# One attention and scan kernel: the drain after the last unit becomes part of the planned order

## The chip, the cores and the metric

The kernel runs on one core of a Trainium2 chip. The metric is the device time of one execution in microseconds (us). Before the change it was 2515.1 us, the median of three runs (2513.02 to 2516.12).

Engines are named as in the profile: PE is TensorE (the matmul array), DVE is VectorE, ACT is ScalarE, POOL is GpSimd, SP is SyncE, which here only issues transfers. Each works through its own queue in order, and an instruction at a queue's head that waits holds up everything behind it.

## What is computed

The reference is one layer: cross attention, then a recurrent scan over time, then two additions. Cut to what matters, with 4096 rows of `x`, 3202 rows of context, width 512, 8 heads of 64 and a state of 64:

```python
xn, kn = layernorm(x, g1, beta1), layernorm(ctx, g1, beta1)
x = x + mha(xn, kn, W_qkv, b_qkv, W_o, b_o)          # softmax over 3202 keys
U = (layernorm(x, g2, beta2) @ W_in.T + b_in) @ Bmat  # 4096 x 64
def step(s, u_t):
    s = silu(s @ A.T) + u_t
    return s, s
_, states = lax.scan(step, zeros(64), U)              # 4096 steps, one after the other
x = x + states @ Cmat
return x + program_probs.mean() @ W_prog.T + b_prog
```

Everything is float32.

## The kernel before

**The attention.** The rows are cut into 8 blocks of 512 (`NQB`), each with 4 pairs of heads (`NC`) and 2 halves of 256 rows: 64 units. A unit runs over 13 double chunks of keys (`NDC`). For each chunk PE makes the scores `s` (L605), ACT copies them to `p` (L618), DVE keeps a running maximum `top` (L633). Once the unit's maximum is known, PE turns it (`tt`, L641), DVE reduces it (`m`, L648) and PE spreads it over the partitions (`mb`, L656). Then, chunk by chunk, DVE subtracts it (`less`, L664), ACT takes the exponential (L674), POOL adds the weights up (`acc`, L682) and PE multiplies by the values (`po`, L691). In the very last unit some chunks aren't added by POOL: PE sums them with a product by ones (`pd`, L708). The variable `PE_SUMS` says which; before, chunks 2, 4, 6, 8, 10 and 12.

**The order of the work.** All of this is entered into a `Plan` (L54) as pieces. A piece has a name, an engine, an estimated cost in ns, the pieces it comes after, a due time, and the buffers that it takes and gives back. `Plan.order` (L92) plays the pieces through with these costs. Whenever an engine is free, it takes the piece that is due first among those that are ready and have buffers, and the list that results is the order in which instructions are issued. So the planner's costs and due times decide only the order on each engine; the chip then runs each queue as fast as its waits allow.

**The scan.** The 4096 steps are cut into 256 stretches of 16 (`L`). The stretches lie side by side, in two groups of 64 states on the 128 partitions, so one matmul by `a_t` advances all of them by a step. A sweep (L1062) is 16 such steps: PE adds the recurrent part to `z` (L1072), ACT takes a tanh (L1085), DVE multiplies it with `z` to `h` (L1086). The inputs' part of `z` comes four steps at a time from `terms` (L1053 to L1057). Sweep a starts every stretch from nothing. Sweep b starts each from the end state that sweep a found for the stretch before it, and from its states POOL forms `s` (L1096), PE the rows `states @ Cmat` (`products`, L1102, tiles `py`, `py_b`, `py_o`), ACT, POOL and DVE join them with the rows that were fetched from DRAM (`row`, L1109 to L1112), and SP stores them. At the end the end states of both sweeps are compared (`differ`, L1128 to L1134); should they differ, a branch repeats the sweeps.

**The last 256 rows.** They belong to the last units, so their attention is finished last, and they have a small scan of their own with stretches of 8 steps: `last_rows` (L1175) takes the last unit's output `o`, multiplies by `W_o` (`py`, L1170), adds the residual (`x_l`, L1187), normalizes (DVE statistics, three short POOL operations, ACT), turns the rows (`tp_yl`, L270), forms the scan's inputs (`pu_l`, L1198), and then makes 24 small steps (`zl`, L1250, tanh L1252, product L1253).

**The drain, before.** The plan ends with the last unit's pieces, the fetches of the rows for sweep b (`row<-x1d`, L1020, 32 transfers on SP's queue) and the first three parts of the last rows' product. After that the order is written by hand. `finish_last` (L716) sums `acc`, takes the reciprocals and scales `o`. Then two generators are advanced in turn: for each `yield` of `last_rows` one step of `main_scan`, which is sweep a and then sweep b with its products, delayed by a step:

```python
for _ in last_rows(ws[len(units) - 1]):
    next(scan, None)
for _ in scan:
    pass
last_outputs("a")
```

In sweep a, PE also gets filler matmuls: two products of a tile of zeros per step (L1078), bf16, 512 columns, whose result nobody reads. Each product of sweep b is one matmul of 512 columns for each of the two groups of states (64 partitions each).

Of the kernel before, what the change touches and what calls it, by code (L numbers as in the profile page):

```python
# [20 lines left out]
P = 128  # L21
# [142 lines left out]
def xattn_ssm_kernel(  # L164
# [37 lines left out]
    zeros = const.tile([P, H], BF16, name="zeros")  # L202
    nc.gpsimd.memset(zeros, 0.0)
# [512 lines left out]
    def finish_last(w):  # L716
        Q, hp, half = w["at"]
        o = op.tile([P, QU], F32, tag="o", name=f"o_{Q}_{hp}_{half}", bufs=12)
        o_t[Q, hp, half] = o
        nc.scalar.copy(o, w["po"][:, 0, :])  # L720
        sums(w["pd"], w["acc"], CK, False, True)
        yield
        rd = op.tile([P, QU], F32, tag="rd", name="rd_last", bufs=1)
        for t in range(2):
            nc.vector.reciprocal(
                rd[:, t * P : (t + 1) * P], w["pd"][:, t * P : (t + 1) * P]
            )
            if t == 0:
                yield
        nc.vector.tensor_tensor(o, o, rd, ALU.mult)  # L730
        yield

# [264 lines left out]
    PE_SUMS = range(2, NDC, 2)  # L997
# [64 lines left out]
    def sweep(start, end, fill=0):  # L1062


        before = None
        for j in range(L):
            if j == 0:
                terms(0, start)
            h = sv["h"][j % 3]
            z = sv["z"][:, j // 4 % 2, j % 4, :]  # L1070
            if before is not None:
                nc.tensor.matmul(z, a_t, before, start=False, stop=True, skip_group_check=True)  # L1072
            if j % 4 == 1 and j + 4 < L:
                terms(j // 4 + 1, None)
            elif fill:

                for _ in range(fill):
                    nc.tensor.matmul(  # L1078
                        sv["fill"], zeros[:, :P], zeros, start=True, stop=True
                    )  # L1080
            if j == 0 and start is None:
                nc.vector.memset(h, 0.0)
            else:
                th = sv["th"][j % 2]
                nc.scalar.activation(th, z, AF.Tanh, scale=0.5)  # L1085
                nc.vector.scalar_tensor_tensor(h, th, 1.0, z, ALU.add, ALU.mult)  # L1086
            before = h
            if j < L - 1:
                yield j, h
        nc.vector.tensor_tensor(end[:, 1:], h, u[:, L - 1, :], ALU.add)  # L1090
        nc.vector.tensor_copy(end[NS:, 0:1], end[:NS, NCK : NCK + 1])
        yield j, h
# [6 lines left out]
    def products(j, s):  # L1099
        for v, n in enumerate(counts):  # L1100
            r = slice(v * NS, (v + 1) * NS)
            nc.tensor.matmul(sv["py"][j % 2][v], s[r, :], sv["c2"][r], start=True, stop=True)  # L1102

    def outputs(j):

        py, t, y = sv["py"][j % 2], rows[j], sv["y"][:, j % 2, :]
        n = counts[1]
        if j % 3 < 2:
            nc.scalar.activation(y, py[1], AF.Copy, scale=0.5)  # L1109
            nc.gpsimd.tensor_tensor(t[:n, 1, :], y[:n], t[:n, 1, :], ALU.add)  # L1110
        for v in range(1 if j % 3 < 2 else 2):
            nc.vector.scalar_tensor_tensor(  # L1112
                t[: counts[v], v, :], py[v][: counts[v]], 0.5, t[: counts[v], v, :],
                ALU.mult, ALU.add,
            )
        nc.sync.dma_start(outr[0, j], t[:, 0, :])
        nc.sync.dma_start(outr[1, j, :n], t[:n, 1, :])
# [7 lines left out]
    def differ(new, old, n, bad):  # L1125

        top, df, ok = sv["top"], sv["df"][:, :n], sv["ok"][:, :n]
        nc.vector.tensor_tensor(df, new, old, ALU.subtract)  # L1128
        nc.vector.tensor_scalar(ok, df, top, None, ALU.is_le)
        nc.vector.tensor_scalar(df, df, -1.0, None, ALU.mult)  # L1130
        nc.vector.tensor_scalar(df, df, top, None, ALU.is_le)
        nc.vector.tensor_tensor(ok, ok, df, ALU.mult)
        nc.vector.tensor_reduce(bad, ok, AX.X, ALU.add, negate=True)
        nc.vector.tensor_scalar(bad, bad, float(n), None, ALU.add)  # L1134

    def main_scan():
        ends = sv["end0"], sv["end1"]
        sv["z"] = ps_s.tile([P, 2, 4, NCK], F32, tag="s", name="z")
        for end in ends:
            nc.vector.memset(end[:NS, 0:1], 0.0)  # L1140
# [4 lines left out]
        yield  # L1145
        for _ in sweep(None, ends[1], 2):
            yield

        s = None
        for j, h in sweep(ends[1][:, :NCK], ends[0]):  # L1150
            if j:
                products(j - 1, s)
            s = states(j, h)
            if j > 1:
                outputs(j - 2)
            yield
        products(L - 1, s)
        largest(ends[0][:, 1:])
        outputs(L - 2)
        yield  # L1160
        differ(ends[0][:, 1:], ends[1][:, 1:], NCK, sv["bad"])
        yield
        outputs(L - 1)
        yield

    def last_products(cs):

        for c in cs:
            for g in range(2):
                nc.tensor.matmul(  # L1170
                    sv["py"][0][g], o_t[NQB - 1, c, 1][:, g * P : (g + 1) * P], wo[:, c, :],
                    start=(c == 0), stop=(c == NC - 1),
                )

    def last_rows(w):  # L1175

        yield from finish_last(w)
        last_products([NC - 1])
        yield
        tiles = range(2)  # L1180
        x1s, scaled, tps, pus = [], [], [], []
        ul, hw, hl, sl, th = (sv[k] for k in ("ul", "hw", "hl", "sl", "thl"))

        def x1_(g):
            x1 = xp_.tile([P, H], F32, tag="x1", name=f"x1_l{g}")
            x1s.append(x1)
            nc.vector.tensor_tensor(x1, sv["py"][0][g], xl[g], ALU.add)  # L1187

        def turn(g):
            tps.append(transposes(ps_m, "m", xhs[g], P, f"yl{g}"))  # L1190

        xns = [sv["xn"][:, g, :].rearrange("p (c k) -> p c k", c=NC) for g in tiles]

        def steps_(g):
            pu = ps_m.tile([P, P], F32, tag="m", name=f"pu_l{g}")
            pus.append(pu)
            for c in range(NC):
                nc.tensor.matmul(  # L1198
                    pu[g * NS : (g + 1) * NS], wc[:, c, :], xns[g][:, c, :],
                    start=(c == 0), stop=(c == NC - 1),  # L1200
                )

        def kept(g):
            hs = slice(g * NS, (g + 1) * NS)
            nc.vector.tensor_scalar(
                ul[hs, PRE + 1 :], pus[g][hs], bu[hs], 2.0, ALU.add, ALU.mult
            )

        xhs = []
        x1_(0)  # L1210
        yield
        scaled.append(normalize(x1s[0], P, "yl0", later=True))
        yield
        x1_(1)
        yield
        xhs.append(scaled[0]())
        scaled.append(normalize(x1s[1], P, "yl1", later=True))
        yield
        turn(0)
        yield  # L1220
        xhs.append(scaled[1]())
        nc.scalar.copy(xns[0], tps[0])
        yield
        turn(1)
        steps_(0)
        yield
        nc.scalar.copy(xns[1], tps[1])
        kept(0)
        nc.vector.tensor_copy(ul[NS:, : PRE + 1], ul[:NS, P:])
        yield  # L1230
        steps_(1)
        for g in tiles:
            nc.gpsimd.tensor_tensor(xl[g], x1s[g], modb, ALU.add)
            nc.sync.dma_start(x1d[LAST + g * P : LAST + (g + 1) * P, :], xl[g])
        yield
        kept(1)

        zl = ps_m.tile([P, PRE // LT + 1, P], F32, tag="m", name="zl")
        for i in range(PRE // LT + 1):
            nc.tensor.matmul(  # L1240
                zl[:, i, :], a_t, ul[:, i * LT : i * LT + P], start=(i == 0), stop=True,
                skip_group_check=True,
            )
        yield
        before = None
        for t in range(PRE + LT):
            i, j = divmod(t, LT)
            z = zl[:, i, j::LT]
            if before is not None:
                nc.tensor.matmul(z, a_t, before, start=False, stop=True, skip_group_check=True)  # L1250
            h = (hl if i == PRE // LT else hw)[:, j::LT]
            nc.scalar.activation(th, z, AF.Tanh, scale=0.5)  # L1252
            nc.vector.scalar_tensor_tensor(h, th, 1.0, z, ALU.add, ALU.mult)  # L1253
            if t == PRE:

                nc.vector.tensor_tensor(sv["st"], hw[:, LT - 1 :: LT], ul[:, PRE :: LT][:, : P // LT], ALU.add)
            before = h
            yield
        nc.vector.tensor_tensor(sl[:, 1:], hl, ul[:, PRE + 1 :], ALU.add)

# [252 lines left out]
```

## Time and profile before

| | us |
|---|---|
| median of three runs | 2515.1 |
| the profiled execution | 2515.3 |
| its span | 2513.5 |
| PE busy | 2418.6 (96%) |
| DVE busy | 2087.6 (83%) |
| POOL busy | 2066.7 (82%) |
| ACT busy | 1922.3 (76%) |
| last `mb`, start | 2410.8 |
| first step of sweep a, its `terms` on PE | 2436.5 |
| first `z` of sweep b | 2462.7 |
| `nbad`, the last operation before the branch | 2507.3 |

The span runs from the first to the last recorded instruction, and the execution's own time is 1.8 us longer. The profile is of one execution, taken on the chip. Its page gives busy times, the granted clock of PE, the chain of work that ended last (followed back from the last instruction), and the costliest groups of instructions by line. The trace behind it can be asked for the timeline of an engine, for waits, and for busy times by windows. `L705` stands for line 705 of the kernel; `po<-p,v` for output and inputs.

### The profile page before, as it was taken

What the parts mean: (1) busy time and instruction counts of PE and PEld (TensorE: products, weight loads), DVE (VectorE), ACT (ScalarE), POOL (GpSimd) and SP (SyncE); (2) the same over time, 40 slices, a digit from 0 to 9 for tenths busy, and PEclk for the clock granted to TensorE, in tenths of its full rate; (3) what the DMA queues carried; (4) which work ended last, traced back from release to release, by engine and by line L of the source; (5) the groups of instructions that cost most, each with busy time, mean ns of one, the idle gap of its engine ahead of it and who ended that gap; (6) DMA issues with size and microseconds to landing.
All of it is one profiled execution on the core that took longest, in us unless ns stands there. A gap on an engine that the chain in (4) does not pass through costs nothing.

```text
span 2513.5 us, 43994 instructions
## 1 busy us (share of the span) xinstructions
PE 2418.6 (96%) x16390; PEld 1409.1 (56%) x16392; DVE 2087.6 (83%) x2242; ACT 1922.3 (76%) x2373; POOL 2066.7 (82%) x1195
## 2 busy tenths in 40 slices
PE   7999899999999999999999999999999999999987
PEld 3444555655565555655565556555565556555543
DVE  2220699999999989899999999999989899999964
ACT  2222588878987898788987898789878888888852
POOL 1110299989998999899998999899989999899963
PEclk9999999999999999999999999999999999999998
DMA  3422322112211222122211221222212221233364
GB/s 120 131 99 79 88 64 62 45 48 68 66 56 53 66 66 66 49 62 85 64 49 43 68 78 46 60 67 67 58 48 67 74 64 53 83 115 118 107 165 144
DMA packets 178035, 189.21 MB, mean 75 GB/s; under 512 B 14252, under 2 KB 151256, under 8 KB 177818
## 3 DMA queue, kind: packets, MB, share of 16 engines
q1 hardware_dynamic: 173270, 178.67, 23.7%
q10 hardware_dynamic: 4548, 7.67, 1.0%
q8 instruction: 133, 2.18, 0.4%
q14 instruction: 84, 0.69, 0.1%
HBM read 156.40 MB, written 29.89 MB: 74 GB/s over the span
## 4 chain that ended last, share of the span: by engine, by line
PE 38%; DVE 22%; POOL 17%; issue 13%; ACT 6%; DMA 2%; SPq 1%; ACTq 0%; POOLq 0%; DVEq 0%
POOL acc L682 15%; DVE top L633 12%; PE s L605 12%; PE po L691 9%; DVE p L664 6%; ACT p L618 3%; PE pv L534 3%; PE pk L560 3%; PE pq L294 3%; PE pa L900 2%; ACT p L674 2%; PE tt L641 1%; POOL both L747 1%; PE pd L753 1%; DMA cx<-in_ctx_dram 1%
## 5 line engine op out<-in xcount | busy, mean ns | idle before, releaser
L682 POOL TENSOR_TENSOR acc<-p,acc 122x1024 f32<-122x1024 f32 (+1 forms) x698 | 1653.0, 2368 | 60.7 <-ACT p L674 17.9
L664 DVE TENSOR_TENSOR p<-p,mb 123x1024 f32<-123x1024 f32 (+2 forms) x832 | 991.7, 1208 | 23.2 <-PE mb L656 23.2
L674 ACT ACTIVATE p<-p 123x1024 f32<-123x1024 f32 (+2 forms) x832 | 875.4, 1058 | 138.9 <-DVE p L664 134.2
L618 ACT COPY p<-s 123x1024 f32<-123x1024 f32 (+2 forms) x832 | 829.6, 1006 | 168.4 <-PE s L605 121.6
L605 PE MATMUL s<-q,k 64*123 64x256 f32 (+2 forms) x6656 | 911.1, 398 | 25.2 <-DVE top L633 15.0
L691 PE MATMUL po<-p,v 123*64 123x256 f32 (+2 forms) x6656 | 877.5, 390 | 6.6 <-ACT p L674 4.7
L633 DVE TENSOR_TENSOR top<-s,top 123x1024 f32<-123x1024 f32 (+1 forms) x640 | 777.3, 1215 | 11.5 <-ACT p L618 9.3
L605 PEld LDWEIGHTS s<-q,k 64*123 64x123 f32 (+2 forms) x6656 | 574.9, 182 | 337.7 <-DVE top L633 115.9
L691 PEld LDWEIGHTS po<-p,v 123*64 123x64 f32 (+2 forms) x6656 | 423.5, 136 | 357.9 <-issue 145.5
L682 POOL TENSOR_TENSOR acc<-p,p 124x1024 f32<-124x1024 f32 x64 | 152.3, 2380 | 121.2 <-DMA k<-kd 73.8
L633 DVE TENSOR_TENSOR top<-s,p 124x1024 f32<-124x1024 f32 x64 | 78.2, 1222 | 99.3 <-ACT p L618 66.3
L294 PE MATMUL pq<-xn,wq 128*128 128x256 f32 x512 | 126.7, 390 | 0.0
L243 POOL TENSOR_SCALAR ve_c<-mv_c 123x1 f32<-123x1 f32 (+2 forms) x26 | 6.1, 233 | 145.7 <-DVE mv_c L236 117.8
L900 PE MATMUL pa<-wo,o 128*128 128x512 f32 x240 | 116.9, 609 | 0.0
L504 DVE COPY ct<-tp_c 128x492 f32<-128x492 f32 (+2 forms) x13 | 8.7, 672 | 123.3 <-PE tp_c L270 123.3
L294 PEld LDWEIGHTS pq<-xn,wq 128*128 128x128 f32 x512 | 92.2, 189 | 31.6 <-issue 21.2
L568 ACT ACTIVATE ks<-pk,bias 128x492 f32<-128x492 f32 (+3 forms) x28 | 18.0, 643 | 118.6 <-PE pk L560 58.4
L534 PE MATMUL pv<-wv,ct 128*123 128x512 f32 (+2 forms) x208 | 99.0, 621 | 0.0
L560 PE MATMUL pk<-ct,wk 128*128 128x492 f32 (+3 forms) x224 | 89.1, 550 | 0.0
L747 POOL TENSOR_TENSOR both<-acc 124x512 f32<-124x512 f32 x63 | 80.8, 1283 | 3.0
L648 DVE TENSOR_REDUCE m<-tt 128x4 f32<-128x496 f32 x64 | 42.9, 671 | 42.7 <-PE tt L641 42.7
L534 PEld LDWEIGHTS pv<-wv,ct 128*123 128x123 f32 (+2 forms) x208 | 39.1, 196 | 46.0 <-issue 45.1
(196 smaller groups left out, 1486.3 us busy)
## 6 DMA issues: line engine op xcount, KB each, us to landing
k<-kd SPq DMA_DIRECT2D x324, 123.0 KB
v<-vd SPq DMA_DIRECT2D x324, 123.0 KB
k<-kd SPq DMA_DIRECT2D x108, 124.0 KB
v<-vd SPq DMA_DIRECT2D x108, 124.0 KB
xr<-in_x_dram SPq DMA_DIRECT2D x32, 256.0 KB
x1d<-xr SPq DMA_DIRECT2D x32, 256.0 KB
x<-in_x_dram SPq DMA_DIRECT2D x28, 256.0 KB
cx<-in_ctx_dram SPq DMA_DIRECT2D x18, 246.0 KB
```

The costliest lines, as they stand in the source:

```text
L294: nc.tensor.matmul(pq[:, half * QU : (half + 1) * QU], wq[:, i, hp * P : (hp + 1) * P], xns[half][:, i, :], start=(i == 0), stop=(i == NC ...
L534: nc.tensor.matmul(pv[:n, :H], ct[:, i, o : o + n], wv[:, i, :], start=(i == 0), stop=(i == NC - 1),)
L560: nc.tensor.matmul(pk[:, :n_g], wk[:, i, hp * P : (hp + 1) * P], ct[:, i, :n_g], start=(i == 0), stop=(i == NC - 1),)
L605: nc.tensor.matmul(s[:n, a, b, :], kts[(*w["at"][:2], c)][r, b * n : (b + 1) * n], q[r], start=True, stop=True,)
L618: nc.scalar.copy(t[:n], w["ps"][c][:n])
L633: nc.vector.tensor_tensor(w["top"][:n], s[:n], before[:n], ALU.max)
L664: nc.vector.tensor_tensor(t[:n], t[:n], w["mb"][:n].unsqueeze(2).to_broadcast([n, 2, 2, QU]), ALU.subtract,)
L674: nc.scalar.activation(t[:n], t[:n], AF.Exp)
L682: nc.gpsimd.tensor_tensor(w["acc"][:n], t[:n], before[:n], ALU.add)
L691: nc.tensor.matmul(w["po"][a * HD : (a + 1) * HD, 0, :], vts[(*w["at"][:2], c)][:n, b, a * HD : (a + 1) * HD], t[:n, a, b, :], start=(c == ...
L747: nc.gpsimd.tensor_tensor(w["both"], acc[:, :, 0, :], acc[:, :, 1, :], ALU.add)
L900: nc.tensor.matmul(v["pa"], o_t[Q, c, t // 2][:, t % 2 * P : (t % 2 + 1) * P], wo[:, c, :], start=(c == 0), stop=(c == NC - 1),)
```

## The change

The hand-written part goes. `finish_last`, `main_scan` and the interleaving loops are replaced by pieces of the plan with names, costs, predecessors and due times, so that the planner decides their order together with the last unit's softmax. In particular:

- sweep a is entered with a pace of 1500 ns a step and a due time of three `STEP` (2600 ns each) behind the last unit's scores. Its only predecessor is `start`, which makes the scan's tiles ready; nothing ties it to the end of the last unit
- the last unit's sums, reciprocals and scaling, the last rows and their small scan, and sweep b at 1900 ns a step follow with due times from 16 `STEP` on
- `PE_SUMS` becomes chunks 4, 8 and 12; POOL adds 2, 6 and 10
- a product of sweep b is entered in two parts of 256 columns, so it is four matmuls instead of two, between which other pieces can stand
- the scaling of the last `o`, the last product by `W_o` and the comparisons are cut into smaller pieces
- the fillers and the tile of zeros are removed

```diff
-    PE_SUMS = range(2, NDC, 2)
+    PE_SUMS = (4, 8, 12)
+    A_PACE, B_PACE = 1500, 1900
...
-    def sweep(start, end, fill=0):
...
-            elif fill:
-                for _ in range(fill):
-                    nc.tensor.matmul(
-                        sv["fill"], zeros[:, :P], zeros, start=True, stop=True
-                    )
...
+    def sweep(k, start, end, d=0, pace=0, after=()):
...
+        for j in range(L):
+            q = j // 4
+            if j % 4 == 0:
+                free = [(k, "h", 4 * q - 5)] if q > 1 else list(after)
+                yield (k, "terms", q), "PE", 950, partial(terms_, q), free, d - 3 * pace if q else d
+            if j or start is not None:
+                if j:
+                    yield (k, "z", j), "PE", 300, partial(z_, j), [(k, "terms", q), (k, "h", j - 1)], d
+                yield (
+                    (k, "tanh", j), "ACT", 280, partial(tanh_, j),
+                    [(k, "z", j) if j else (k, "terms", 0)], d + 400,
+                )
+                free = [("states", j - 3)] if j > 2 and start is not None else []
+                yield (k, "h", j), "DVE", 290, partial(h_, j), [(k, "tanh", j)] + free, d + 800
...
+            d += pace
+        yield (k, "end"), "DVE", 450, last_, [(k, "h", L - 1)], d
...
+    def last_unit(plan, w, n, d):
...
+        plan.add("l.copied", "ACT", 370, copied, [("product", n, NDC - 1)], d, ["o_"])
+        plan.add("l.summed", "PE", 860, summed,
+                 [("add", n, last)] + [("sums", n, c) for c in PE_SUMS], d, [], [], "product")
+        for t in range(2):
+            plan.add(("l.inverse", t), "DVE", 950, partial(inverse, t), ["l.summed"], d + t,
+                     [] if t else ["wide"], [("m", ("sums", n, PE_SUMS[0]))])
+            plan.add(("l.over", t), "DVE", 290, partial(scaled_, t), ["l.copied", ("l.inverse", t)], d + t)
...
+        for p in sweep("a", None, "end1", d + 3 * STEP, A_PACE, ["start"]):
+            plan.add(*p)
+        d += 16 * STEP
+        last_unit(plan, ws[n], n, d)
+        last_rows(plan, d)
+        for p in sweep("b", "end1", "end0", d + STEP, B_PACE, [("a", "end")]):
+            plan.add(*p)
...
+            for part in range(2):
+                plan.add(("products", j, part), "PE", 590, partial(products_, j, part),
+                         [("states", j), *free[j % 2]], e + 1000 + part)
...
-        sv["fill"] = sv["py"][1][0]
-        for _ in last_rows(ws[len(units) - 1]):
-            next(scan, None)
-        for _ in scan:
-            pass
-        last_outputs("a")
-        differ(sv["sl"][:, : P : LT], sv["st"], P // LT, sv["badl"])
```

The computation stays the same, apart from the order of the sums in the last unit's denominators. The branch that repeats the sweeps is rewritten to the new form of `sweep`, with the same steps.

## The prediction

> **What bounds the kernel now.** I read the page first. PE is busy 96% of the span, and the first 2400 us are the planned order, which the change leaves alone: by the listing of both built programs, each engine's instructions agree up to the last unit's softmax. So only the last 110 us matter, and there I read the chain of work that ended last:
>
> ```profile
> 2434.89 1.73 PE pd L708 x16
> ...
> 2440.56 0.44 DVE o L730
> ...
> 2458.03 0.94 PE zl L1240 x6
> ...
> 2462.74 0.49 PE z L1056 x2
> ...
> 2495.33 0.39 PE py_b L1102
> ...
> 2502.22 2.13 PE py_a L1267 x4
> ```
>
> Columns: start, length, engine, tile, line. Four stages follow from it. S1, from the end of the last `mb` (2411.85, PE's timeline) to the end of the sum over `acc`, the last group of `pd` (2436.5): 24.6 us. S2, sweep a and the first half of the last rows, to sweep b's first `z` (2462.74): 26.3. S3, sweep b with its products, to the end of the last product (2495.72): 33.0. S4, to the end of `nbad` (2507.5): 11.8. Then 6.0 to the end of the span.
>
> Next the timeline, for the price of a step:
>
> ```profile
> 2443.94 0.49 PE L1072 MATMUL z<-scan,a_t 128*128 128x128 f32 x2 [0.26 <-DVE scan L1086]
> ...
> 2445.12 0.49 PE L1072 MATMUL z<-scan,a_t 128*128 128x128 f32 x2 [0.26 <-DVE scan L1086]
> ...
> 2470.35 0.40 PE L1250 MATMUL zl<-scan,a_t 128*128 128x16 f32 x2
> 2470.60 0.47 PE L1072 MATMUL z<-scan,a_t 128*128 128x128 f32 x2
> 2470.99 0.69 PE L1102 MATMUL py_b<-c,scan 64*128 64x512 f32 x1
> ```
>
> A bare sweep step (`z`, tanh, product, next `z`) takes 2445.12 − 2443.94 = 1.18. On a busy PE a `z` takes 0.25 when the next matmul has the array's same shape, but 0.39 (2470.60 to 2470.99) when the next one uses half of it: 0.14 for the change of shape. On POOL's own timeline five additions to `acc` take 12.17 from 2419.01, 2.43 each.
>
> Last, PE by windows (window, length, busy, instructions, granted clock, DMA share, GB/s):
>
> ```profile
> 2401.57:2404.98 3.41, 1.66 (x12) 1.00 0.22 76
> 2404.98:2408.39 3.41, 3.08 (x10) 0.50 0.20 69
> ...
> 2439.11:2442.52 3.41, 2.40 (x8) 1.00 1.06 252
> ...
> 2493.72:2497.13 3.41, 2.06 (x10) 1.00 0.76 255
> ```
>
> The clock halves after a window with 1.66 or 2.06 busy (the next one's clock is 0.50 both times), not after one with 2.40.
>
> **The change part by part.** Ahead of S1 nothing moves the path: `mb` stands behind one group of `py` in both orders. The dropped memset of `zeros` has no row of its own; the nearest, a DVE memset, takes 0.17, on a POOL that is idle for most of the first 150 us: nothing, at most 0.2.
>
> *Sweep a into S1.* PE gains 15 `z` x 0.25 = 3.75 and four terms, 0.66 + 3 x 0.87 = 3.3. It loses three of six chunk sums, 3 x 0.87 = 2.6 (their chunks go to POOL). Changes of shape rise from 7 to 25, 18 x 0.14 = 2.5. PE's work grows by 6.9: 24.6 + 6.9 = 31.5, to 2443.4.
>
> Each step also puts a wait into three queues: `z` on PE (the next `po` stands behind), tanh on ACT (the next exp), the product `h` on DVE (the next subtraction). In the new order five `h` stand between the subtractions and ten behind the last. The subtractions end at 2411.89 + 13 x 1.13 + 5 x 0.21 + 0.8 (`rd`) + 0.35 (`o`) = 2428.8, 1 us later than now. From there `z`7 to `z`15 take seven steps with a `po` between them, 0.25 + 0.14 + 0.86 + 0.14 = 1.39, longer than the bare 1.18 and so PE's, and one with terms, 2.04 as at 2445.12 to 2447.16: 11.8. Then `z`15 and three groups, 0.4 + 2.6: 2443.9. The two sums agree; with half a microsecond for imperfect fit, 2444.4. **S1: +8.0.** The cover: POOL does nine additions, its last ending at 2419.01 + 8 x 2.43 = 2438.5 where now it ends at 2431.2. The sum over `acc` is due at 2443.5, so these 7.3 us are hidden by 5; were sweep a free, S1 could still not end before 2439.4, +2.9.
>
> Tanh among exps: both orders hold one load of ACT's function set, at the start, so no switch is paid. ACT is busy 14.6 of the 26 us from 2411 and gets 15 x 0.28 = 4.2.
>
> *S2 disappears.* Sweep b's first `z` follows the sum directly. The 26 filler matmuls, 0.215 each, go with it. **−26.3.**
>
> *S3 takes the last rows.* Now: 16 `z` (4.0), terms (3.3), 16 products of 0.92 (14.7), 16 small steps `zl` (3.8), 31 changes of shape (4.3), sum 30.1, and 2.9 of waiting, mostly for DVE's joins `row` (two in a row, 1.28). After: besides, the last `py` 1.9, transposes 0.9, `pu` 2.0, terms of the small scan 0.8, two small steps more, 48 changes: 38.0, +7.9. Half-width products: a block becomes four of 256 columns, the shape of the scores, 16 records in 1.99, 8 in 0.99 with its change of shape; the full width took 1.06 with its own. I take no difference; worse by 0.14 a step they would cost 2.2, better by 0.07 they would give 1.1.
>
> The waiting grows. DVE holds both reciprocals (0.95 each) and the scalings back until the sum is there: `o` at 2446.9. From `o` to the terms of the small scan it took 17.0 (2441.0 to 2458.0); the rows' bare chain (`py` 0.95, `x1` 0.68, statistics 0.87, POOL 1.25, 0.81, transposes 0.5, 0.56, `pu` 1.0, the second tile 3.2 behind, 0.8) is some 11; middle 14, so 2460.9 = 16.5 after S3's start. By the new order five `z` of sweep b but only four products stand before that. Behind it PE still has 12 products (10.6), 11 `z` (2.75), terms 1.7, 18 small steps 4.3, some 36 changes 5.0: 24.4; and 11 steps wait, at twice today's 0.18 a step since 1.6 small steps now stand in DVE's queue per step: 4.1. S3: 16.5 + 24.4 + 4.1 = 45.0. **+12.0.**
>
> SP: the 32 fetches keep their place (2415 to 2441.6, DMA share 1.07); the stores moved ahead start near 2450, so they collide with nothing, and 7.7 MB have 40 us where they had 30. The two stores of `xr` stand among them and nobody waits.
>
> *S4.* Five small steps at 1.10 (2499.70 to 2500.80), the states 0.3, `py_a` 2.1, two joins and a remnant of the comparison 1.6, `pbad` and `nbad` 0.6: 10.1. The first comparison, seven operations, 2 us on DVE, no longer stands between two small steps (1.62 idle before `zl`), and most of the second lies beside `py_a`. **−1.7.**
>
> Sum: 8.0 − 26.3 + 12.0 − 1.7 = −8.0. The profiled execution took 2515.3 (span 2513.5), within 0.2 of the median of three, 2515.1. 2515.3 − 8.0 = **2507.3 us**.
>
> **Rules weighed.** The Trainium skill, "TensorEngine Tiling (Array Packing)", Key Properties, says that a change of tiling mode drains the array, which speaks against half-width products with `z` and `zl` in between. The row prices the drain at 0.14; 35 more changes make 4.9, counted above. The rule gives no figure; the gain would be gone at 0.14 + 8.0/35 = 0.37 a change, which no row shows.
>
> "TensorE: Matmul & The Clock Gate" (Why this matters for your kernels) fears idle gaps above some 3 us. By it nothing happens here, fillers or not: no gap of this walk reaches 2 us. By the row the clock fell after gaps no longer than 1.53, in a window half busy. The row decides: the stretch around 2447 to 2452, where sweep b waits for the last rows, may fall. It is a rival below.
>
> **The rivals.** *PE alone decides.* The queues add no waiting beyond today's: +6.9 − 26.3 + 7.9 − 1.7 = −13.2, **2502.1**. For it: sweep steps with fillers between ran at 1.18. Against: 17 us from `o` to the small scan.
>
> *The clock halves once in early S3.* The fall at 2404.98 made `po` 1.98 for 1.08, `py` 3.78 for 1.98, `mb` 1.06 for 0.64: 3.1. Then −4.9, **2510.4**. For it: only four products in 16 us. Against: `pu`, `py` and the terms are dense there, and 2.40 of 3.41 was enough.
>
> *Slower: the coupled queues.* A late `h` on DVE holds `z`, the matmuls behind it, the joins behind those and so the next `h`. Place: the 9 steps at the end of S1 and the 16 of S3. Each 0.1 us more a step costs 2.5. From 0.32 a step the gain is gone, at 0.52 the kernel takes 2515.3 − 8.0 + 13.0 = **2520.3**. For it: a step with one `pu` group in between took 1.94 (2454.60 to 2456.54), 0.55 over mine. Against: that step also had a filler, and PE was simply full.
>
> That the change does not do what it says is excluded: the listing shows the `z` between the `po`.
>
> **How the numbers follow.** Likeliest 0.53 (its own range 2505 to 2510), PE alone 0.17, the clock 0.20, slower 0.08, something unseen 0.02. About 0.2%, 5 us, can be told from no change: faster, below 2510.3, holds the first two and a little under half of the third, 0.76; same 0.16; slower 0.08. The range 2502.0 to 2512.5 leaves out the slower case and half of the edges.
>
> **What would show it.** `acc`'s sum ending near 2444 with POOL's last addition near 2438; sweep b's first `z` right behind it; terms of the small scan near 2461; the last product near 2489.5; granted clock 1.00 from 2412 to there. Wrong would be: `z` in S1 over 1.6 apart, POOL ending last, S3 above 48, or a window at 0.50 between 2447 and 2461.

## The result, and the profile after

The changed kernel takes 2509.7 us, the median of 20 runs (2505.8 to 2512.18); the kernel before 2514.8, the median of 20 (2512.38 to 2516.82). The ratio is 0.9979, with a 95% interval of 0.9973 to 0.9986: 5.1 us faster, where 7.8 were forecast. The profiled execution took 2511.05, with a span of 2509.2; that is 4.25 less than the profiled execution of before.

The chain of the changed kernel, at the places that were shown of the kernel before (start, length, engine, tile, line):

```profile
2444.13 0.89 PE pd L706 x8
...
2446.73 0.24 DVE o L1197
...
2461.78 0.86 PE zl L1264 x6
...
2490.89 1.08 PE py L1102 x4
...
2499.04 2.13 PE py_a L1325 x4
```

The order is turned round. Sweep a is gone from behind `pd`. From the end of `o` to the small scan's terms it is 14.8 us, where it was 17.0, and the 30.2 us from these terms to the end of the last product hold sweep b, its products and the small steps together.

The stages, cut as in the prediction, from PE's and DVE's timelines. S1 runs from the end of the last `mb` to the end of the sum over `acc`, S2 to sweep b's first `z`, S3 to the end of the last product, S4 to the end of `nbad`. The experiments, named below, stand in the same table:

| kernel | S1 | S2 | S3 | S4 | `mb` to `nbad` | median |
|---|---|---|---|---|---|---|
| before | 24.8 | 26.1 | 33.0 | 11.7 | 95.6 | 2514.8 |
| forecast | 32.8 | 0 | 45.0 | 10.0 | 87.6 | 2507.3 |
| after | 33.5 | 0 | 47.0 | 11.0 | 91.5 | 2509.7 |
| sweep a late | 28.2 | 24.9 | 42.5 | 5.9 | 101.5 | 2521.9 |
| six sums on PE | 37.0 | 0 | 44.7 | 11.0 | 92.8 | 2515.0 |
| products whole | 33.5 | 0 | 41.2 | 18.2 | 92.9 | 2509.8 |
| work in sweep b | 33.5 | 0 | 44.5 | 11.0 | 88.9 | 2507.8 |
| the same, and at the end | 33.5 | 0 | 44.4 | 11.2 | 89.0 | 2508.4 |
| before, no fillers | 24.9 | 26.8 | 35.9 | 11.7 | 99.3 | 2522.7 |
| late rows on DVE | 33.5 | 0 | 48.1 | 10.0 | 91.6 | 2510.3 |
| work in sweep b, late rows | 33.5 | 0 | 43.4 | 10.2 | 87.0 | 2505.6 |
| the same, and at the end | 33.5 | 0 | 43.4 | 9.4 | 86.2 | 2504.9 |
| work, late rows, two sums | 32.6 | 0 | 43.4 | 10.2 | 86.1 | 2505.5 |

The forecast row adds the prediction's differences to the row of before (its S2 would come out at −0.2). With six sums, sweep b starts ahead of the sum, so S3 is counted from the sum's end. The stages are those of one profiled execution, the median is that of all runs. They need not move alike: the last `mb` ends anywhere from 2407 to 2414 in these profiles, in a part of the program that is the same in all of them, so stages are compared by their lengths and not by absolute times. The experiments were timed in three groups (the first four, the next four, the last three, as they stand below), each with the kernel before, whose medians were 2514.9, 2514.2 and 2515.1. So differences of medians between groups are good to about 1 us, and the ratio to the kernel before, given with its 95% interval, compares better.

S1 is the length that repeats best, 33.5 in seven kernels. S3 carries the difference. PE by windows there (window, length, busy, instructions, granted clock, DMA share, GB/s):

```profile
2449.35:2452.76 3.41, 1.64 (x12) 1.00 0.00 0
2452.76:2456.18 3.42, 3.42 (x16) 0.60 0.45 143
...
2476.65:2480.07 3.42, 2.50 (x18) 1.00 0.42 148
2480.07:2483.48 3.41, 3.41 (x18) 0.60 0.73 237
```

Twice in S3 the clock falls to 0.50 for the length of one such stretch (the first time from 2453.4 to 2456.8; a window that mixes it with full clock shows 0.60). Each time the stretch ahead has waits in it: 1.28 and 0.49 in the first, for DVE's `h` and POOL's states, and 0.53 and 0.39 in the second.

```profile
2451.56 0.49 PE L1052 MATMUL z<-scan,a_t 128*128 128x128 f32 x2 [1.28 <-DVE scan L1065]
2452.54 0.70 PE L1102 MATMUL py<-c,scan 64*128 64x256 f32 x4 [0.49 <-POOL scan L1096]
```

Before, no window from 2412 to 2497 was below 1.00.

And the end, all engines between 2492 and 2496, where a small step has to wait 1.80:

```profile
2492.73 1.26 POOL L1119 TENSOR_TENSOR row<-y_l,row 112x512 f32<-112x512 f32 x1 [2.97 <-ACT scan L1279]
2492.76 0.18 DVE L1282 SCALAR_TENSOR_TENSOR scan<-scan,zl 128x16 f32<-128x16 f32 x1 [0.24 <-ACT scan L1279]
2492.85 1.29 DVE L1153 TENSOR_TENSOR scan<-scan,scan 128x128 f32<-128x128 f32 x1
...
2495.41 0.61 PE L1276 MATMUL zl<-scan,a_t 128*128 128x16 f32 x2 [1.80 <-DVE scan L1282]
```

The comparison's multiplication (L1153) takes 1.29, though the comparison's other operations of its size take 0.23 to 0.29, and it ends 0.15 behind POOL's addition. The Trainium skill, "SBUF — State Buffer" (SBUF: two separate sides), says that a DVE operation with two SBUF inputs and a GpSimd operation that reads SBUF share a pair of ports, which the first comer holds to its end. The row agrees, and an experiment below takes the addition away. Behind the multiplication DVE still has the rest of the comparison and a join of 0.69, so the small step's product comes at 2495.18 and the next `zl` at 2495.41.

### The profile page after: what moved, and what is told of

It reads as the page before. It is cut to its first block, busy times and chain, and to the rows that moved or that the text cites. A ratio compares the mean times of both kernels' runs of the same rounds, so it can differ in the third digit from the quotient of the medians.

```text
span 2509.2 us, 44018 instructions
## 1 busy us (share of the span) xinstructions
PE 2414.7 (96%) x16406; PEld 1411.4 (56%) x16406; DVE 2089.5 (83%) x2243; ACT 1920.8 (77%) x2373; POOL 2071.5 (83%) x1197
## 4 chain that ended last, share of the span: by engine, by line
PE 38%; DVE 22%; POOL 16%; issue 13%; ACT 7%; DMA 2%; SPq 1%; ACTq 0%; POOLq 0%; DVEq 0%
POOL acc L680 14%; DVE top L631 13%; PE s L603 12%; PE po L689 9%; DVE p L662 6%; ACT p L616 3%; PE pv L532 3%; PE pq L292 3%; PE pk L558 3%; PE pa L881 2%; ACT p L672 2%; PE tt L639 1%; POOL both L728 1%; SPq L571 1%; PE pd L734 1%
## 5 line engine op out<-in xcount | busy, mean ns | idle before, releaser
L680 POOL TENSOR_TENSOR acc<-p,acc 122x1024 f32<-122x1024 f32 x701 | 1658.8, 2366 | 60.9 <-ACT p L672 17.6
L631 DVE TENSOR_TENSOR top<-s,top 123x1024 f32<-123x1024 f32 (+1 forms) x640 | 778.1, 1216 | 12.2 <-ACT p L616 10.3
L532 PE MATMUL pv<-wv,ct 128*123 128x512 f32 (+2 forms) x208 | 99.3, 623 | 0.0
```

The lines of the kernel that those rows point to most:

```text
L532: nc.tensor.matmul(pv[:n, :H], ct[:, i, o : o + n], wv[:, i, :], start=(i == 0), stop=(i == NC - 1),)
L631: nc.vector.tensor_tensor(w["top"][:n], s[:n], before[:n], ALU.max)
L680: nc.gpsimd.tensor_tensor(w["acc"][:n], t[:n], before[:n], ALU.add)
```

## The experiments

**Sweep a behind the sum.** Undoes the move alone.

```diff
-        for p in sweep("a", None, "end1", d + 3 * STEP, A_PACE, ["start"]):
+        for p in sweep("a", None, "end1", d + 3 * STEP, A_PACE, ["l.summed"]):
```

> Sweep a's first terms wait for the sum over acc instead of for the scan's tiles alone, so the sweep no longer stands beside the last unit's products; the rest of the plan stays. If hiding sweep a is the gain: S1 shrinks from 33.4 us to POOL's last addition and one group, 27.9 + 1.0 = 28.9 (-4.5); S2 comes back with sixteen steps of 1.18 and the end, about 20, beside the last rows; S3 gives most of its added 14 back, since the last rows and the start of the small scan then lie in S2, say -12. Sum +3.5: 2513, between 2511 and 2516. Rival: the planning of the last rows and of sweep b is what gains, sweep a's place is nothing: 2509.7 within 1.

2521.9 us, ratio to the kernel before 1.0031 (1.0020 to 1.0042): 12.2 above the changed kernel and slower than the kernel before. Sweep a's place is worth more than the whole gain; without it the planned order loses. This kernel has no fillers either, and an experiment below takes them out of the kernel before: that takes 2522.7 (1.0033), the same within the intervals. So what else the change does gains nothing that shows here. S1 came at 28.2 (28.9 expected), and what ends it is POOL:

```profile
2437.79 1.61 PE L706 MATMUL pd<-acc,ones 124*64 124x256 f32 x8 [4.71 <-POOL acc L680]
```

PE idles 4.71 for the additions that three sums fewer have given to POOL: the prediction's 5 us of cover, seen from its other side. The floor that it gave for S1 with a free sweep a was 2.9 above before; this is 3.4 above, with the sum itself slow at 1.61. S2 took 24.9 instead of 20: the sweep's steps share PE and DVE with the last rows, and the clock is at 0.50 from 2439 to 2441 and again from 2459.3 to 2474, where a step takes 1.48 instead of 1.18:

```profile
2459.33 0.79 PE L1052 MATMUL z<-scan,a_t 128*128 128x128 f32 x2 [0.56 <-DVE scan L1065]
...
2460.81 0.80 PE L1052 MATMUL z<-scan,a_t 128*128 128x128 f32 x2 [0.45 <-DVE scan L1065]
```

S3 and S4 gave back 9.6 of the 12 expected. So part of the 12.2 is the clock, which in the kernel before the fillers held.

**Six sums on PE.**

```diff
-    PE_SUMS = (4, 8, 12)
+    PE_SUMS = range(2, NDC, 2)
```

> Six chunks of the last unit's denominators are summed on PE as before, and POOL adds the other six. If PE's content sets S1: three more groups of 0.87 with POOL ending some 7 us earlier, S1 +2.6, 2512.3. Rival: the coupled queues or POOL's last addition set S1, and PE has room: 2509.7 or a little less.

2515.0 us (0.9998, 0.9989 to 1.0007): 5.3 slower than the changed kernel, where 2.6 were expected. In its profile S1 is 3.5 longer: three sums of 0.87 are 2.6, and about half of the other 0.9 is sweep b's first two `z` and its first terms (1.5 together), which the planner here puts ahead of the sum over `acc` (`z` at 2439.97, the sum at 2443.33), less a group of `po` (1.0) that it puts behind. So S1 is PE's content, as forecast, and POOL has room. From `mb` to `nbad` it is 1.3 longer than after, and that profile is the fastest of the eleven runs (2508.1); their mean granted clock was 0.990, against 0.992 for the changed kernel. The rest of the 5.3 may thus be the clock in the other runs; no profile shows it.

**Products whole.** The products of sweep b are entered as one piece of 512 columns again.

```diff
-            for part in range(2):
-                plan.add(("products", j, part), "PE", 590, partial(products_, j, part),
+            for part in range(1):
+                plan.add(("products", j, part), "PE", 1060, partial(products_, j, part),
...
-            products(j, sv["s"][j % 2], slice(part * QU, (part + 1) * QU))
+            products(j, sv["s"][j % 2])
```

> A row's product by c is entered whole again, two matmuls of 512 columns and 1.06 us. The prediction took no difference between two halves and one block: 2509.7 within 0.5. If halves cost 0.14 a step for their extra change of shape, this gains 2.2 (2507.5); if their value is that z and zl stand between them, the whole block holds each such matmul back by 0.5 at half of the steps: some 4 worse, 2513.7.

2509.8 us (0.9977, 0.9967 to 0.9987), 0.1 from the changed kernel. The forecast of no difference holds, but not because nothing moves: S3 is 5.8 shorter and S4 7.2 longer. With whole products fewer small steps fit into S3: eleven stand behind the last product instead of five, most of them alone, at half clock:

```profile
2490.83 0.61 PE L1276 MATMUL zl<-scan,a_t 128*128 128x16 f32 x2 [0.84 <-DVE scan L1282]
2491.93 0.61 PE L1276 MATMUL zl<-scan,a_t 128*128 128x16 f32 x2 [0.49 <-DVE scan L1282]
2493.03 0.61 PE L1276 MATMUL zl<-scan,a_t 128*128 128x16 f32 x2 [0.49 <-DVE scan L1282]
```

Such a bare small step costs 1.10. S3 is 5.8 longer with the six steps that half-width products make room for, 0.97 a step, so the room brings little. Not all of the 5.8 is the steps': this profile's S3 has only the first of the two falls of the clock.

**More work for PE in sweep b, first try.** It repeated terms block by block, in the four regions of a bank.

> Sweep b's steps 1 and 2 each repeat the next four blocks of terms (0.87 us of PE), steps 9 to 15 two blocks each (0.43), with the values they have anyway: work for PE in the two stretches before the clock fell in S3 (1.64 and 2.50 of 3.41 us busy). Clock theory: with 1.7 and 0.9 us more of work in them those windows no longer let the clock fall; each fall of 3.4 us cost up to 1.7, the one at the end 0.5, so S3 is 3 to 4 shorter, less 2 for late fillers that delay a full PE: 2508, and no window of S3 at 0.50. Rival: waits and PE's own content set S3 and the falls lie in slack: the fillers only cost, 2511 to 2513.

11104 us. The end states of the sweeps then differed and the branch that repeats the sweeps ran. The Trainium skill, "PSUM — Partial Sum Buffer" (The four PSUM rules), has the likely reason: a matmul that starts a group clears the marks of its whole bank, so the next `z` overwrites the other regions' terms instead of adding to them. The next run, which issues whole groups only, does not enter the branch; it differs in its steps too, so the reason is likely and not shown. Up to `nbad` the trace still tells the order's time: S3 45.3 instead of 47.0 and no fall of the clock in it, although PE has some 4.7 us more to do (2 x 0.87 and 7 x 0.43). And in the branch, at clock 0.50, `z` stands at 2506.64, 2508.13 and 2509.61: a bare sweep step of 1.49, against 1.18 at full clock.

**The same with whole groups.** Steps 1, 2, 11 and 15 each issue one group of terms more.

```diff
                 start=False, stop=True, skip_group_check=True,
             )
+            if k == "b" and j in (1, 2, 11, 15):
+                q = min(j // 4, 2)
+                nc.tensor.matmul(
+                    sv["z"][:, (j // 4 + 1) % 2], a_t, u[:, 4 * q + 3 : 4 * q + 7, :],
+                    start=True, stop=True, skip_group_check=True,
+                )
```

> Four whole groups of terms (0.87 us each) are issued once more in sweep b, behind steps 1, 2, 11 and 15, into a bank that the step does not read and with the values it gets anyway: work for PE in the stretches ahead of the three falls of the clock, the whole computation kept. Clock theory: S3 stays at clock 1.00 and takes some 45 us instead of 47.0, the first zl being no later: 2507.5 to 2508.5. Rival: the waits for DVE and POOL set S3: the fillers cost what they push, 0 to 2 us, 2510 to 2512.

2507.8 us (0.9972, 0.9962 to 0.9982). The intervals of the two ratios overlap; the stage decides. S3 is 44.5 instead of 47.0, with 3.5 us more work on PE, and its windows in the same places read:

```profile
2449.35:2452.76 3.41, 3.05 (x16) 1.00 0.23 80
2452.76:2456.18 3.42, 3.37 (x24) 1.00 0.43 145
...
2476.65:2480.07 3.42, 3.42 (x25) 1.00 0.74 237
2480.07:2483.48 3.41, 3.37 (x20) 1.00 0.74 258
```

Both falls are gone. The mean granted clock of its runs was 0.993, against 0.992 after (20 runs) and 0.993 before (24). The clock theory holds: holding both falls off brings 2.5, net of the work that it takes, most of which must lie in PE's waits.

**The same, and work at the end.** 256 columns more behind each of the last five small steps.

> As the run with four more groups of terms in sweep b, and behind each of the last five small steps a matmul of 256 columns (0.43 us) into the bank that sweep b has done with. If the clock alone made the small steps 1.10 apart and py_a 2.08: five steps gain 0.2 each (zl 0.61 to 0.40) and py_a 1.0, S4 11.1 to 9.1, 2506. Rival: the steps are latency of ACT and DVE and py_a lies beside the comparison: no more than the run without them.

2508.4 us (0.9976, 0.9966 to 0.9986): nothing gained. A wait of 1.40 for DVE still stood between two of the steps, the window 2486.89 to 2490.31 held 2.03 of work, and the clock fell behind it; `py_a` took 2.08 as ever. The rival's number came out, but not for its reason, as a later run shows.

**The kernel before without its fillers.**

```diff
-        for _ in sweep(None, ends[1], 2):
+        for _ in sweep(None, ends[1], 0):
```

> The kernel before without its 26 filler matmuls in sweep a, nothing else. Clock theory: in S2 PE then has 0.25 to 0.5 us of work in 1.2, the clock falls there, a bare step takes 1.5 instead of 1.18 and the last rows' products twice their time: sixteen steps 0.3 each and 2 for the rows, some 2521. Rival: the fillers only filled, waits set S2 and the steps full with fillers get shorter: 2513 to 2515.

2522.7 us, 8.5 above the kernel before (1.0033, 1.0021 to 1.0045); mean granted clock 0.988. In its profile:

```profile
2448.20:2451.61 3.41, 1.89 (x11) 1.00 0.31 91
2451.61:2455.02 3.41, 2.72 (x8) 0.58 0.20 75
...
2461.85:2465.26 3.41, 1.45 (x10) 1.00 0.00 0
2465.26:2468.67 3.41, 2.61 (x8) 0.58 0.00 0
2468.67:2472.09 3.42, 3.42 (x8) 0.50 0.00 0
```

The second fall takes in the first products of sweep b, and S3 is 2.9 longer. The four stages hold 3.7 of the 8.5; the profiled run, 2519.4, was among the faster of its six (2516.8 to 2526.9), and where the rest goes no profile shows. So the fillers did hold the clock in the kernel before, and the change, which drops them, needs the denser order for that as well: S1 does it, S3 does not.

**Late rows on DVE.** POOL adds no row behind row 12.

```diff
-        spread = j % 3 < 2
+        spread = j % 3 < 2 and j < 13
```

> Rows 13 and 15 are joined on DVE alone, so POOL has no addition of 1.26 behind step 12. If POOL's late additions are what S3's end and S4 wait for: the last states no longer stand behind one (1.2 of idle PE before the last product) and the comparison's operation takes 0.29 instead of 1.29; less two joins of 0.69 on DVE, a gain of about 1: 2508.7. Rival: DVE's order is what holds the small steps, and gets two joins more: 2510 to 2511.

2510.3 us (0.9979, 0.9971 to 0.9988): no gain. But its parts moved: the comparison's multiplication took 0.28, S4 is 1.0 shorter, and S3 is 1.1 longer, because in this profile the clock stood near 0.50 from 2479 on. Which of the two belongs to the edit, the next run separates.

**Work in sweep b, and late rows on DVE.** Both edits together.

> Both edits that touched a wait of their own: the four groups of terms in sweep b (1.9 better alone) and rows 13 and 15 joined on DVE (nothing alone, in a profile whose clock stood at 0.50 for 9 us ahead of the last product). If POOL's additions still cost and the clock hid it: the wait of 1.9 between two small steps goes, 2506.5. Rival: DVE is what the end waits for either way: 2507.8.

2505.6 us (0.9965, 0.9953 to 0.9977). Against the same work without the rows: S3 −1.1, S4 −0.8, ratio −0.0007 (1.8 us; the intervals overlap, the stages decide). The multiplication now reads

```profile
2488.64 0.28 DVE L1159 TENSOR_TENSOR scan<-scan,scan 128x128 f32<-128x128 f32 x1
```

and the longest wait of a small step behind it is 0.99, not 1.93. POOL's additions did hold the end.

**Also with work at the end.**

> The same, and 256 columns of work behind each of the last five small steps. Without the wait of 1.4 at POOL's addition the windows of S4 hold over 2.1 us of PE work each, so the clock should not fall before py_a: small steps 0.9 instead of 1.1 apart and py_a 1.0 shorter, 2505. Rival: the clock falls all the same, as in the run with these matmuls alone: no better than without them, 2506.5 to 2508.

2504.9 us (0.9959, 0.9945 to 0.9972), the lowest median here, and the one ratio whose interval lies wholly below that of the changed kernel. S4 is 0.8 shorter, and `py_a` is not at half clock:

```profile
2496.22 1.13 PE L1336 MATMUL py_a<-c,scan 64*128 64x512 f32 x4 [0.29 <-DVE scan L1302]
```

1.0 less in `py_a`, as expected, but of that DVE's comparison, which lies beside it, takes a part back: a wait of 1.36 follows where it was 0.78.

**And with two sums.** Work in sweep b, late rows, and chunks 6 and 12 alone summed on PE.

> As the first of these three, with two chunks of the last unit summed on PE (6 and 12) and one more addition on POOL. If PE's content sets S1: one group and a change of shape less, -1.2, while POOL's last addition, 2.4 later, ends some 1 us ahead of the sum's new place: 2505.3. Rival: POOL's chain then ends last, or the steps of sweep a set the tail: 2506.5 or worse.

2505.5 us (0.9961, 0.9948 to 0.9975), the same as without it (2505.6). S1 is 0.9 shorter, just the group that went (0.87), where 1.2 were expected with its change of shape. POOL's last addition did not end last. In the medians the step is too small to be seen.

## Why the prediction was right, and where it was off

The direction and the source of the gain are right. The size was forecast 2.4 us too good; 2509.7 lies inside the likeliest case's own range (2505 to 2510), near its edge. It lies nearer to the rival "the clock halves once in early S3" (2510.4), and that fall came. By steps, against the profile of before:

- **S2, −26.3:** −26.1. Sweep b's first `z` starts at 2444.93, as the sum over `acc` ends:

```profile
2443.96 1.03 PE L706 MATMUL pd<-acc,ones 124*64 124x256 f32 x8
2444.93 0.49 PE L1038 MATMUL z<-scan,a_t 128*128 128x128 f32 x2
```

The first experiment shows that this is the whole gain, and more. Against the two kernels without fillers and with sweep a behind the sum, the move brings 12 to 13 us. Dropping the fillers, which the prediction priced at nothing beyond their place in S2, costs 8.5 in the old order. The 5.1 is what is left between kernels that differ in both.
- **S1, +8.0:** +8.7. The mechanism is right: PE's content sets it, POOL's last addition ends at 2439.4 (2438.5 forecast) and is covered by 4.6, and S1 goes by one group when a group goes. The miss lies mostly where the steps start: the seventh `z` begins at 2429.70, 1.0 after the last subtraction, because a group of `po` and one of `pd` stand ahead of it on PE; the sum let it begin at once, and allowed half a microsecond in all. The step of `z` and `po` was forecast at 1.39 and takes 1.43.

```profile
2436.04 0.49 PE L1052 MATMUL z<-scan,a_t 128*128 128x128 f32 x2
2436.45 1.08 PE L689 MATMUL po<-p,v 123*64 123x256 f32 x8
2437.47 0.49 PE L1052 MATMUL z<-scan,a_t 128*128 128x128 f32 x2
```

- **S3, +12.0:** +14.0, the term that was mis-sized most. The small scan's terms came 16.8 after its start (16.5 forecast), and the rest took 30.2, not 28.5. With the clock held at 1.00 the two are 15.7 and 28.8, together 44.5 against 45.0, with 3.5 of extra work that lies mostly in PE's waits: the sum itself was good to about 0.5, but it was made at full clock. The prediction had the fall in early S3 as a rival of its own at 3.1 and gave it 0.20; its reason against it, dense work and 2.40 of 3.41 us busy being enough, does not hold: the stretch ahead held 1.64, and a second fall, 27 us later, came behind 2.50. It named a window at 0.50 between 2447 and 2461 as the sign that would prove it wrong, and the profile has it (2453.4 to 2456.8). Its price, 3.1, was taken from a fall of 6.8 us; these last 3.4 each, and holding both off brought 2.5. So the likeliest case's time was nearly met while its assumption on the clock was not; with the clock held in S3 the kernel takes 2507.8, close to the forecast 2507.3.
- **S4, −1.7:** −0.7. The prediction took the first comparison to be out of the small steps' way. It is not: its last piece still stands between two of them, and POOL's addition stretches it by 1.0. Without that S4 is 10.2 (10.0 forecast).
- **Half-width products, 0:** 0.1 in the median, as the balance of −5.8 and +7.2.

The terms miss by 0.7, 2.0 and 1.0 us, all on one side, and by 0.2 in S2: 3.9, the difference between a forecast of 8.0 and the profile's 4.1. In the medians it is 2.7. Three of the prediction's sums are slips: its second sum for S1 gives 2443.6 and not 2443.9, its twelve products in S3 11.0 and not 10.6 at its own 0.92, and PE's work in S3 38.6 and not 38.0. The first two cancel to 0.1; the third moves only the rival "PE alone decides", to 2502.7.

The rival "PE alone decides" is out: PE got 3.5 us more work in sweep b and S3 became shorter. So is the slower one, at 0.5 a step: its place was right, since the waits are there, but S1's steps took 0.04 over the forecast, and S3 with a steady clock took less than forecast.

What stays open is what exactly makes the clock fall. Behind the same 1.64 of work at the same place it fell in the profile after and did not in that of the run with late rows alone, and ahead of S1 the profile after has a window with 1.88 busy that did not lower it:

```profile
2404.98:2408.39 3.41, 1.88 (x16) 1.00 0.31 96
2408.39:2411.81 3.42, 3.42 (x18) 1.00 0.20 70
```

## What to carry to other kernels

Hiding a latency chain beside dense matmuls is worth what the chain took alone, minus its own work on the busiest engine and what then stands in the other chains' queues: here 26 us became 5, and 2.5 of the difference is the clock, which nothing held in S3 any more. When an order is made denser and fillers are dropped, look at the granted clock in the part that did not become dense, and put harmless work there. Read a piece that moves with the engines that run beside it: the comparison was cheap where it had stood, and 1.0 dearer beside an addition on POOL.

## What the runs showed of the hardware

- The clock fell behind waits of 1.28 and 0.49 or of 0.53 and 0.39 within a window, with up to 2.50 of 3.41 us busy; no wait of PE in S1 to S3 of the changed kernel reached the 3 us of the rule that the prediction weighed and set aside. The one wait above it, 4.71 with the late sweep, had a fall behind it too: the sum that takes 1.03 at full clock took 1.61. How long PE is shown as busy does not decide alone: in the run with late rows the clock stayed at 0.50 through three windows of 3.41 busy, filled with products of 64 rows, `z`, and small steps of 16 columns.

```profile
2480.07:2483.48 3.41, 3.41 (x14) 0.50 0.45 154
2483.48:2486.89 3.41, 3.41 (x16) 0.50 0.42 141
2486.89:2490.31 3.42, 3.42 (x14) 0.50 0.42 144
```

- Half the clock made a bare sweep step 1.49 instead of 1.18, and its `z` 0.80 instead of 0.49: most of such a step is not PE.
- A DVE multiplication of two SBUF operands took 1.29 or 0.28, as POOL's addition ran beside it or not. With whole products it was the comparison's multiplication by a constant, with one SBUF tensor as input (L1150), that took 1.24 instead of 0.23 beside such an addition.
